# Two attentions and their neighbours: norms two turns ahead of their transposes, paced additions and paced first weights

## The chip, the cores and the metric

The kernel runs on one core of one Trainium2 chip. The metric is the device time of one execution in microseconds. A core has TensorE (PE; "PEld" is its weight load, which overlaps the products), VectorE (DVE), ScalarE (ACT), GpSimd (POOL) and SyncE (SP). Each engine works through its own list of instructions in order and waits at an instruction until the semaphores it names are reached. SP and POOL here also issue DMA transfers (SP for loads and stores, POOL for the gathers by index).

## The reference

Four layers, each with an attention against a context and a feed-forward part; x has 32 batches of 64 rows of 128 numbers, in float32. What matters here:

```python
# layer 1, feed-forward: each row goes to its two best of 8 experts
weights, indices = jax.lax.top_k(gates, 2)
out = jnp.sum(gathered * softmax(weights)[..., None], axis=2)
# layer 2, attention: 16 heads of 8, with a mask of keys
energy = where(mask == 0, -1e20, einsum('nhqd,nhkd->nhqk', q, k))
attn = softmax(energy / sqrt(8)); out = concat(attn @ v) @ Wo.T + bo
# layer 2, feed-forward: a soft mixture of 64 experts with 32 slots each
logits = einsum('bmd,dnp->bmnp', x, phi)
dispatch = softmax(logits, axis=0); combine = softmax over all (n, p)
y = einsum('bnpd,nde->bnpe', slots, W) + b
# layer 3: the same attention with biases, without the mask
# layer 3, feed-forward: 6 experts, two of them weighed in
h = gelu(einsum('btd,edh->bteh', x, w1)); out = einsum('bteh,ehd,bte->btd', h, w2, w)
# and throughout
x = x + part(_layernorm(x))
```

## The kernel before

**Tiles.** The 2048 rows are 16 tiles of 128 rows, in four groups (`NG` 4) of four tiles (`TG` 4). `X[g]` holds a group, 128 x 4 x 128, on chip from end to end. A norm of a group (`norm`, from L141) is on DVE: 4 statistics, 4 aggregations, 12 operations on 128 x 4 numbers for the reciprocal root, and 4 scalings (L157). `norm_T` (L166, L175) transposes its four tiles on PE and copies the result from PSUM on ACT.

**Attention of layers 2 and 3** (`attention16`). One function makes both, in 19 turns. In turn i, PE makes the scores of tile i (L1522 the mask, L1533), then the transposes of the exponentials of tile i-2 (`turn_e`, L166), then the values of tile i-3 (L1571). DVE takes the largest score of each row (L1542) and subtracts it (L1544), ACT makes the exponential in place (L1545) and copies the transposes (L1556). The scores lie in one of two PSUM tiles of two banks each (`banks2`), so the scores of a tile wait until L1544 of the tile two before is through. The logits of the mixture take the same two.

Beside this, steps for a group are put into a list `later` by turn: the queries of group g (norm and POOL's `add_row`, L793, in turn 4g-3; its transposes in 4g-2; the product with Wq, L1298, and ACT's copy or bias, L1301 and L1303, in 4g-1), the loads of the keys and values of group g+1 in turn 4g (`load_kv`: one load for the values and 16 for the keys, all on SP), the projection of group g in turns 4g+7 and 4g+8 (L777 or L779, L784; it ends with the addition to `X[g]`, L180, on DVE), and from turn 4g+8 on, one to a turn, what the caller gives with `after(g)`. Steps of turns past the last are issued one after the other behind the turns; that part is called the tail here.

- In layer 2, `after` is `first_logits(g)`: norm, an empty turn, transposes, and the first of the mixture's eight chunks of logits (`logits`, L1450 on PE, L1459 on DVE, L1465 and L1469 on ACT).
- In layer 3, `after` is `experts3(g)`: norm, an empty turn, transposes, `gate` (L1930, then some 15 small operations on DVE and an exponential on ACT, L1010), `hidden` (L1949 on PE, the Gelu on ACT, L1956), `weigh` (transposes L1023, copy L1025, products L1963, copies L1966 on ACT and products L1967 on POOL, or L1969 on DVE for the last group) and `project` (L1975, L180, and the store of the result on SP, L1983).

The caller of layer 2 also gives `before`: things to issue ahead of the scores of a turn.

**The gathered outputs of layer 1.** `fetch(g, k)` is one indirect DMA from POOL (L1223): 128 rows of an expert's output, one of eight for a group. `add_up_tokens(g)` adds the eight to `X[g]`, with their weights, on DVE (L1238). Groups 2 and 3 are fetched in the first turns of attention 2 and added in turns 4 and 8. A fetch is `paced`: it carries a wait on the last score product issued so far (`pe_at`).

**The first weights of the mixture.** `load_experts(c)` loads 8 of the 64 expert matrices, 512 KB, on SP (L1443) into one of three buffers. Chunks 0 and 1 are issued ahead of attention 2, chunk 2 after it.

**Order.** PE's list in the turns is exactly the order in which the function issues it: `in_order` binds each instruction behind the one before. The lists of DVE, ACT, POOL and SP, and PE's list in the tail, are put in order by the framework's planner, which takes the instructions by priority (the order of issue) as its own estimates say that they become ready. An instruction that is issued early can thus stand in DVE's list ahead of one that is ready sooner on the chip.

Of the kernel before, what the change touches and what calls it, by code (L numbers as in the profile page):

```python
# [20 lines left out]
ALU = mybir.AluOpType  # L21
# [30 lines left out]
def tile_layers(ctx: ExitStack, tc: tile.TileContext, io, out):  # L52
    nc = tc.nc
# [54 lines left out]
    def paced(ins):  # L108

        if pe_at[0] is not None:  # L110
            tc.add_manual_dep(
                ins.ins,
                pe_at[0].ins.name,
                mybir.DependencyInfo(mybir.DependencyClass.Sync, mybir.DependencyReason.DATA),
                reason="pace",
            )
# [378 lines left out]
    with tc.tile_pool(name="dtw", bufs=1, reuse_waits="tile") as dp:  # L495
# [131 lines left out]
        for i in range(S):  # L627
# [12 lines left out]
            if i % 16 == 15:  # L640
                q = i // 16
# [588 lines left out]
            )  # L1230
        )

    def add_up_tokens(g):
        wk = share.pop(g)[1]
        yg = ys.pop(g)
        for t in range(TG):
            for c in range(2):
                nc.vector.scalar_tensor_tensor(  # L1238
                    X[g][:, t, :], yg[c][:, t, :], wk[:, t, c : c + 1], X[g][:, t, :], ALU.mult, ALU.add
                )  # L1240


# [197 lines left out]

    def load_experts(c):
        wsm[c] = fa.tile([P, 8, D], F32, tag="wsm", name=f"wsm{c}", bufs=3)
        nc.sync.dma_start(wsm[c], io["W"][c * 8 : c * 8 + 8].rearrange("n p e -> p n e"))  # L1443

    def logits(c, g):

        ps = banks2(f"l{c}_{g}")
        psv = ps.rearrange("p (t s) -> p t s", t=TG)
        for k in range(TG):
            nc.tensor.matmul(  # L1450
                psv[:, k, :],
                xT2[g][:, k * P : (k + 1) * P],
                phi[:, c * CS : (c + 1) * CS],
                start=True,
                stop=True,
            )
        at = slice(g * TG, (g + 1) * TG)
        if c == 0:
            nc.vector.tensor_reduce(nmr[:, c, at], psv, AX.X, ALU.max, negate=True)  # L1459
        else:  # L1460
            rm = small.tile([P, TG], F32, tag="f2_rm", name=f"rm{c}_{g}")
            nc.vector.tensor_reduce(rm, psv, AX.X, ALU.max, negate=True)  # L1462
            nc.vector.tensor_tensor(nmr[:, c, at], rm, nmr[:, c - 1, at], ALU.min)  # L1463
        lg = fa.tile([P, TG, CS], F32, tag="lg", name=f"lg{c}_{g}", bufs=7)
        nc.scalar.copy(lg.rearrange("p t s -> p (t s)"), ps)  # L1465
        e = fa.tile([P, TG, CS], F32, tag="e", name=f"e{c}_{g}", bufs=4)
        for k in range(TG):
            t = g * TG + k
            nc.scalar.activation(e[:, k, :], psv[:, k, :], AF.Exp, bias=nmr[:, c, t : t + 1])  # L1469
        lgs[c, g], es[c, g] = lg, e  # L1470

        if g == 1:
            m = fa.tile([P, TG, CS], F32, tag="cm", name=f"cm{c}")
            nc.vector.tensor_tensor(m, lgs[c, 0], lg, ALU.max)
            cmx[c] = m
        elif g > 1:
            nc.vector.tensor_tensor(cmx[c], cmx[c], lg, ALU.max)
# [13 lines left out]
    def first_logits(g):  # L1491
        def normalise():
            xl2[g] = norm(g, "n5")

        def turn_over():
            xT2[g] = norm_T(g, "n5", xl2[g])[1]

        return [normalise, lambda: None, turn_over, lambda: logits(0, g)]

    load_experts(0)  # L1500
    load_experts(1)

    def attention16(ly, q16, wo, bv=None, mask=None, after=None, before={}):

# [3 lines left out]
        with tc.tile_pool(name=f"a{ly}", bufs=2, reuse_waits="tile", side="right") as aw:  # L1512
# [77 lines left out]

            for g in range(NG):
                if g:
                    for k, step in ((-3, normalise), (-2, turn_over), (-1, lambda g: queries(g, aw, "q"))):
                        later.setdefault(4 * g + k, []).append(lambda step=step, g=g: step(g))
                if 0 < g < NG - 1:
                    later.setdefault(4 * g, []).append(lambda g=g: load_kv(ly, g + 1, kv16[ly]))

                later.setdefault(4 * g + 7, []).append(
                    lambda g=g: later.setdefault("po", project_steps(g, os_[g], wo, f"a{ly}po{g}", bv))[0]()
                )  # L1600
                later.setdefault(4 * g + 8, []).append(lambda: later.pop("po")[1]())
                for k, step in enumerate(after(g)):
                    later.setdefault(4 * g + 8 + k, []).append(step)
# [17 lines left out]
    with tc.tile_pool(name="mask", bufs=1, reuse_waits="tile", side="right") as mp:  # L1621
        mi = mp.tile([P, NT, S], I32, name="mi")
        nc.sync.dma_start(mi, io["mask"].rearrange("(t p) k -> p t k", p=P))
        mb = mp.tile([P, NT, S], BF16, name="mb")
        nc.vector.tensor_scalar(mb, mi, 0.0, -1e20, ALU.is_equal, ALU.mult)
        identb = mp.tile([P, P], BF16, name="identb")
        nc.vector.tensor_copy(identb, ident)
        attention16(2, q2, wat[:, 7, :], mask=(identb, mb), after=first_logits,
            before={
                1: lambda: [fetch(2, k) for k in range(4, 8)],  # L1630
                2: lambda: [fetch(3, k) for k in range(4)],
                4: lambda: [fetch(3, k) for k in range(4, 8)] + [add_up_tokens(2)],
                8: lambda: add_up_tokens(3),
            },
        )

    kv_stack.close()
# [280 lines left out]
    def experts3(g):  # L1918
        v = {}

        def normalise():
            v["xl"] = norm(g, "n7")

        def turn_over():
            v["xT"] = norm_T(g, "n7", v["xl"])[1]

        def gate():
            ps = bank(f"z{g}")
            for t in range(TG):
                nc.tensor.matmul(  # L1930
                    ps[:, t * 6 : t * 6 + 6], v["xT"][:, t * P : (t + 1) * P], pw, start=True, stop=True
                )
            q = fp.tile([P, TG, 6], F32, tag="q", name=f"q{g}")
            nc.scalar.activation(
                q.rearrange("p t e -> p (t e)"), ps[:, : TG * 6], AF.Tanh, scale=1.0 / 0.3
            )
            pr = fp.tile([P, TG, 6, 6], F32, tag="pr", name=f"pr{g}")
            nc.vector.tensor_tensor(pr, _bc(q, 2, 6), _bc(anchors, 1, TG), ALU.mult)
            lg = fp.tile([P, TG, 6], F32, tag="lg", name=f"lg3_{g}")
            nc.vector.tensor_reduce(lg, pr, AX.X, ALU.add)  # L1940
            nc.vector.tensor_scalar(lg, lg, -6.0, 0.5, ALU.add, ALU.mult)
            nc.vector.tensor_scalar(lg, lg, rt, None, ALU.mult)
            v["w"] = top2(lg, 6, con[:, C_T6 : C_T6 + 36], fp, f"tk3_{g}")[1]

        def hidden():
            hw = v["hw"] = fp.tile([P, 3, 512], F32, tag="hw", name=f"hw{g}")
            for c in range(3):
                ps = bank(f"h3_{g}_{c}")
                nc.tensor.matmul(  # L1949
                    ps,  # L1950
                    w1[:, 2 * c : 2 * c + 2, :].rearrange("p e f -> p (e f)"),
                    v["xT"],
                    start=True,
                    stop=True,
                )
                nc.scalar.activation(hw[:, c, :], ps, AF.Gelu_apprx_tanh)  # L1956

        def weigh():
            wT = weights_T(v["w"], 6, fp, f"tk3_{g}", nc.scalar.copy)
            for c in range(3):  # L1960

                ps = bank(f"w3_{g}_{c}")
                nc.tensor.matmul(ps, sel[:, c * P : (c + 1) * P], wT, start=True, stop=True)  # L1963
                if g < NG - 1:
                    wh = fp.tile([P, 512], F32, tag="wh", name=f"wh{g}_{c}")
                    nc.scalar.copy(wh, ps)  # L1966
                    nc.gpsimd.tensor_tensor(v["hw"][:, c, :], v["hw"][:, c, :], wh, ALU.mult)  # L1967
                else:
                    nc.vector.tensor_tensor(v["hw"][:, c, :], v["hw"][:, c, :], ps, ALU.mult)  # L1969

        def project():
            ps = bank(f"o3_{g}")
            for t in range(TG):
                for c in range(3):
                    nc.tensor.matmul(  # L1975
                        ps[:, t * D : (t + 1) * D],
                        v["hw"][:, c, t * P : (t + 1) * P],
                        w2[:, c, :],
                        start=(c == 0),
                        stop=(c == 2),  # L1980
                    )
            add_to(g, ps)
            nc.sync.dma_start(o_rows[g], X[g])  # L1983

        return [normalise, lambda: None, turn_over, gate, hidden, weigh, project]

    kv16[3] = kv_buffers(3, ctx)
    for g in range(2):
# [106 lines left out]
```

## Time and profile before

| | us |
|---|---|
| median of 3 runs | 1115.15 |
| lowest and highest | 1106.98, 1124.36 |
| the profiled execution, its own time | 1120.74 |
| its span in the trace | 1119.0 |
| mean granted clock of PE | 0.88 |
| layer 1's experts end, attention 2 begins | about 445 |
| attention 2, last values end | about 560 |
| mixture, 8 chunks | about 582 to 950 |
| attention 3, its last values end | 1075 |

All times in the trace count from the start of the span. The page first gives each engine's busy time as a share of the span, then the span in 40 slices (28 us each): a digit is the busy share in tenths, and PEclk is the share of its clock that PE was granted. In the timeline a line has its start, its duration, engine, line of code, operation, tiles (written <- read), shapes and how often; in brackets stands how long the engine had been idle and what ended that ("issue": nothing that the profile shows; "remote": a semaphore whose sender it does not know). The windows view has, for each stretch, the length and then each engine's busy time with its number of instructions.

### The profile page before, as it was taken

Reading aid. Unit: us, or ns where it says so; the run is one execution under the profiler, and the core shown is the slowest. Engines: PE = TensorE matmul, PEld = TensorE weight load, DVE = VectorE, ACT = ScalarE, POOL = GpSimd, SP = SyncE. Lnnn points to the kernel's source line nnn. Section 1 sums busy time; section 2 is a strip of 40 time slices with the busy share of each in tenths; the row PEclk is TensorE's granted clock in tenths of the full one; section 3 lists DMA queues with packets and bytes.
Section 4 is the critical chain, followed back from the end, with each engine's and each line's share of the span. In section 5 each row is a group of like instructions: output and inputs, shape, how many; then the busy total and the mean of one; then the engine's idle time right before and its main releaser. Section 6 shows DMA issues by size and latency. Waiting matters only on the chain.

```text
span 1119.0 us, 26304 instructions
## 1 busy us (share of the span) xinstructions
PE 930.6 (83%) x10816; PEld 689.7 (62%) x10816; DVE 766.3 (68%) x2098; ACT 576.9 (52%) x987; POOL 151.7 (14%) x176
## 2 busy tenths in 40 slices
PE   5687679976789998597955989999999998697887
PEld 3455543455657776254644778888888887364554
DVE  8796897767555355456657876887788856867543
ACT  5544526664243454344525775776766733265552
POOL 3500020001053652500000000000000000300111
PEclk9867979989579999778867999999999999598887
DMA  6734030013312231310000000000000000220000
GB/s 229 169 123 151 35 138 8 20 45 102 107 47 46 69 71 52 103 29 4 1 1 1 2 21 2 21 21 2 22 21 2 3 3 3 75 63 2 10 10 19
DMA packets 63124, 51.89 MB, mean 46 GB/s; under 512 B 32663, under 2 KB 53541, under 8 KB 62878
## 3 DMA queue, kind: packets, MB, share of 16 engines
q1 hardware_dynamic: 46958, 29.86, 9.5%
q0 software_dynamic: 4368, 10.92, 3.6%
q10 hardware_dynamic: 11680, 9.44, 2.6%
q8 instruction: 86, 1.41, 0.5%
q14 instruction: 32, 0.26, 0.1%
HBM read 33.51 MB, written 15.60 MB: 44 GB/s over the span
## 4 chain that ended last, share of the span: by engine, by line
PE 56%; DVE 22%; ACT 11%; issue 4%; DMA 4%; POOL 1%; SPq 1%; ACTq 0%; another core or an unknown queue 0%; POOLq 0%; DVEq 0%
PE y L1728 7%; PE po L1747 5%; PE s L1708 4%; PE h L1339 3%; PE a_s L1533 3%; PE y L1361 3%; PE l L1450 3%; PE a_o L1571 2%; DVE lg L1698 2%; PE a_T L166 2%; PE h L893 2%; PE et L1671 2%; PE h1T_T L166 2%; PE w L1963 2%; DVE rm L1462 1%
## 5 line engine op out<-in xcount | busy, mean ns | idle before, releaser
L1728 PE MATMUL y<-wsm,sl 128*32 128x128 f32 x4096 | 118.4, 273 | 2.5 <-ACT sl L1716 2.5
L1728 PEld LDWEIGHTS y<-wsm,sl 128*32 128x32 f32 x4096 | 109.8, 110 | 10.7 <-issue 6.3
L1716 ACT COPY sl<-s 128x1024 f32<-128x1024 f32 x64 | 62.1, 1023 | 69.2 <-PE s L1708 69.2
L1351 ACT ACTIVATE hT<-h1T_T,b_t 128x128 f32<-128x128 f32 x184 | 52.6, 369 | 63.7 <-PE h1T_T L166 53.5
L793 POOL TENSOR_TENSOR X<-X,rows 128x512 f32<-128x512 f32 x8 | 10.2, 1271 | 496.1 <-DVE a3n_xl L157 435.2
L1542 DVE TENSOR_REDUCE a_x<-a_s 128x16 f32<-128x1024 f32 x32 | 39.0, 1217 | 55.9 <-PE a_s L1533 49.7
L1747 PE MATMUL po<-ybuf,cT 128*64 128x136 f32 x1024 | 66.4, 282 | 7.5 <-ACT e L1469 7.3
L1450 PE MATMUL l<-phi,n_xT 128*128 128x256 f32 x256 | 64.7, 408 | 3.5 <-ACT sl L1716 2.8
L1747 PEld LDWEIGHTS po<-ybuf,cT 128*64 128x64 f32 x1024 | 58.3, 137 | 14.2 <-ACT e L1469 8.7
L1708 PE MATMUL s<-lg,n_xl 64*128 64x256 f32 x512 | 65.1, 389 | 0.5 <-ACT e L1469 0.3
L166 PE MATMUL n_T<-con,n_xl 128*128 128x128 f32 x80 | 22.1, 370 | 50.7 <-DVE n_xl L157 30.9
L1556 ACT COPY a_eT<-a_T 128x512 f32<-128x512 f32 x64 | 35.2, 591 | 49.4 <-PE a_T L166 42.8
L1450 PEld LDWEIGHTS l<-phi,n_xT 128*128 128x128 f32 x256 | 50.8, 204 | 15.3 <-issue 4.0
L1761 DVE SCALAR_TENSOR_TENSOR acc<-acc,fac,po 128x128 f32<-128x128 f32 x112 | 31.3, 340 | 41.5 <-PE po L1747 41.5
L1465 ACT COPY lg<-l 128x1024 f32<-128x1024 f32 x32 | 32.6, 1020 | 46.7 <-DVE rm L1462 36.5
L1343 DVE COPY hs<-h 128x512 f32<-128x512 f32 x46 | 31.5, 687 | 35.2 <-PE h L1339 20.3
L1708 PEld LDWEIGHTS s<-lg,n_xl 64*128 64x128 f32 x512 | 47.6, 186 | 12.4 <-issue 5.6
L1204 POOL DMA_INDIRECT xg<-xn_dram,tok_u x46 | 43.7, 951 | 74.9 <-DVE tok_u L1178 30.3
L1339 PE MATMUL h<-w1e,xgT 128*128 x92 | 50.5, 637 | 0.8 <-issue 0.7
L166 PEld LDWEIGHTS a_T<-con,a_e 128*128 128x128 f32 x256 | 32.6, 159 | 29.4 <-issue 20.6
L1545 ACT ACTIVATE a_e<-a_e 128x1024 f32<-128x1024 f32 x32 | 33.8, 1058 | 32.6 <-DVE a_e L1544 26.2
L1469 ACT ACTIVATE e<-l,nmr 128x256 f32<-128x256 f32 x128 | 50.2, 501 | 0.4 <-DVE nmr L1463 0.4
(406 smaller groups left out, 2193.5 us busy)
## 6 DMA issues: line engine op xcount, KB each, us to landing
vd<-vb ACTq DMA_DIRECT2D x8, 576.0 KB
wsm<-in_W SPq DMA_DIRECT2D x8, 512.0 KB
y_dram<-ys SPq DMA_DIRECT2D x10, 256.0 KB
a2vb<-vd SPq DMA_DIRECT2D x4, 576.0 KB
a3vb<-vd SPq DMA_DIRECT2D x4, 576.0 KB
w1e<-in_W POOLq DMA_DIRECT2D x4, 512.0 KB
w2e<-in_W POOLq DMA_DIRECT2D x4, 512.0 KB
ctxT<-in_ctxT SPq DMA_DIRECT2D x4, 256.0 KB
```

Source lines behind the costliest of these rows:

```text
L166: nc.tensor.transpose(ps[:, t * P : (t + 1) * P], a, ident)
L1204: nc.gpsimd.indirect_dma_start(gathered[m][:, t, :], None, xn_dram[h][:], bass.IndirectOffsetOnAxis(ap=phase[h]["tok"][:, j : j + 1], axis=0),
L1339: pe_at[0] = nc.tensor.matmul(po, xgT[m][:, t * P : (t + 1) * P], w1f[:, bass.ds(at_e[m][t], 512)], start=True, stop=True)
L1351: nc.scalar.activation(hT[n][:, c, :], ps[:, c * P : (c + 1) * P], AF.Silu, bias=phase[h]["b1"][:, c, j : j + 1])
L1450: nc.tensor.matmul(psv[:, k, :], xT2[g][:, k * P : (k + 1) * P], phi[:, c * CS : (c + 1) * CS], start=True, stop=True,)
L1469: nc.scalar.activation(e[:, k, :], psv[:, k, :], AF.Exp, bias=nmr[:, c, t : t + 1])
L1542: nc.vector.tensor_reduce(mx, scv, AX.X, ALU.max)
L1556: nc.scalar.copy(eT[:, 4 * half : 4 * half + 4, :].rearrange("p k r -> p (k r)"), ps)
L1708: nc.tensor.matmul(ps[r][:, k * CS : (k + 1) * CS], xl2[g][half, k, :], lgs[c, g][half, k, :], start=True, stop=True,)
L1716: nc.scalar.copy(sl[:, r].rearrange("p q s -> p (q s)"), ps[r])
L1728: nc.tensor.matmul(pyv[(n % 4) * 32 : (n % 4) * 32 + 32, b, n // 4, :], sl[:, b % 2, 2 * h + b // 2, n * 32 : n * 32 + 32], wsm[c][:, n, : ...
L1747: nc.tensor.matmul(pov[r * 64 : r * 64 + 64, k // 2, k % 2, :], cT[:, j, at : at + 64], y[:, 2 * k + r, j, :], start=(j == 0), stop=(j == 1),)
```

## The change

- **Norms.** In `attention16` the norm for the queries of group g comes in turn 4g-4 instead of 4g-3, except for the group named by the new argument `late` (group 2, in layer 2). `first_logits` and `experts3` get a second empty turn between norm and transposes, so that their later steps come a turn later; `experts3` gets one more between `hidden` and `weigh`.
- **Gathered outputs.** `add_up_tokens` takes a function to apply to each addition. Group 2's are issued ahead of turn 5 instead of 4, group 3's ahead of turn 7 instead of 8, and both are `paced`: each addition waits for the last score product before it. The last four fetches are issued ahead of turn 3 instead of 4.
- **First weights.** `load_experts` 0 and 1 are no longer issued ahead of attention 2 but, paced, ahead of its turns 8 and 12.

```diff
-    def add_up_tokens(g):
+    def add_up_tokens(g, when=lambda ins: None):
...
-                nc.vector.scalar_tensor_tensor(
-                    X[g][:, t, :], yg[c][:, t, :], wk[:, t, c : c + 1], X[g][:, t, :], ALU.mult, ALU.add
+                when(
+                    nc.vector.scalar_tensor_tensor(
+                        X[g][:, t, :], yg[c][:, t, :], wk[:, t, c : c + 1], X[g][:, t, :], ALU.mult, ALU.add
+                    )
                 )
...
-        return [normalise, lambda: None, turn_over, lambda: logits(0, g)]
-
-    load_experts(0)
-    load_experts(1)
+        return [normalise, lambda: None, lambda: None, turn_over, lambda: logits(0, g)]
...
-    def attention16(ly, q16, wo, bv=None, mask=None, after=None, before={}):
+    def attention16(ly, q16, wo, bv=None, mask=None, after=None, before={}, late=None):
...
-                    for k, step in ((-3, normalise), (-2, turn_over), (-1, lambda g: queries(g, aw, "q"))):
+                    for k, step in ((-3 if late == g else -4, normalise), (-2, turn_over), (-1, lambda g: queries(g, aw, "q"))):
...
-                4: lambda: [fetch(3, k) for k in range(4, 8)] + [add_up_tokens(2)],
-                8: lambda: add_up_tokens(3),
+                3: lambda: [fetch(3, k) for k in range(4, 8)],
+                5: lambda: add_up_tokens(2, paced),
+                7: lambda: add_up_tokens(3, paced),
+                8: lambda: paced(load_experts(0)),
+                12: lambda: paced(load_experts(1)),
             },
+            late=2,
         )
...
-        return [normalise, lambda: None, turn_over, gate, hidden, weigh, project]
+        return [normalise, lambda: None, lambda: None, turn_over, gate, hidden, lambda: None, weigh, project]
```

More of the change, by code (lines that the diff above doesn't have):

```diff
@@ L1442, in load_experts @@
         wsm[c] = fa.tile([P, 8, D], F32, tag="wsm", name=f"wsm{c}", bufs=3)
-        nc.sync.dma_start(wsm[c], io["W"][c * 8 : c * 8 + 8].rearrange("n p e -> p n e"))
+        return nc.sync.dma_start(wsm[c], io["W"][c * 8 : c * 8 + 8].rearrange("n p e -> p n e"))
     def logits(c, g):
```

## The prediction

> **What bounds the kernel now.** I read the page first: its engine totals and slices, to see which engine is short in the two attentions.
>
> ```profile
> PE 930.6 (83%) x10816; PEld 689.7 (62%) x10816; DVE 766.3 (68%) x2098; ACT 576.9 (52%) x987; POOL 151.7 (14%) x176
> ...
> PE   5687679976789998597955989999999998697887
> ...
> PEclk9867979989579999778867999999999999598887
> ```
>
> PE (TensorE) carries the end, but slices 17 to 22 (attention 2 and the turn into the mixture) and 35 to 40 (attention 3) are mostly short of busy time, of clock or of both. Then the busy time by stretch: attention 2 is 445 to 560 us, its tail to 586; attention 3 starts at 952, and its tail at 1075.
>
> ```profile
> core 0: us, PE busy (x) PEld busy (x) DVE busy (x) ACT busy (x) POOL busy (x), PEclk, DMA share, GB/s
> 445.00:507.00 62.00, 45.94 (x387) 24.42 (x387) 33.26 (x75) 21.92 (x31) 16.46 (x17) 0.78 0.24 65
> 507.00:560.00 53.00, 43.87 (x488) 30.07 (x487) 34.05 (x99) 24.83 (x41) 1.54 (x2) 0.84 0.01 2
> ...
> 975.00:1005.00 30.00, 27.73 (x334) 18.06 (x331) 20.37 (x23) 18.34 (x27) 0.00 (x0) 0.96 0.21 61
> 1005.00:1075.00 70.00, 58.35 (x550) 37.19 (x548) 42.28 (x151) 37.93 (x56) 8.52 (x7) 0.82 0.02 5
> 1075.00:1119.00 44.00, 34.02 (x144) 23.19 (x142) 18.06 (x63) 14.08 (x22) 4.20 (x4) 0.77 0.06 18
> ```
>
> No engine fills these stretches: PE is idle 16, 9, 12 and 10 us of rows 1, 2, 4 and 5, and at 0.77 to 0.84 of its clock while busy. Row 3 shows what turns cost undisturbed: PE 92% busy at 0.96. So the two attentions are bound by short waits of PE, whose order is fixed there, and by the slow clock around them. The timeline says which waits. At the start:
>
> ```profile
> 454.98 0.38 DVE L1238 SCALAR_TENSOR_TENSOR X<-yg,wk,X 128x128 f32<-128x128 f32 x1 [3.18 <-issue]
> 455.28 1.21 DVE L1544 TENSOR_TENSOR a_e<-a_s,a_x 128x1024 f32<-128x1024 f32 x1
> ...
> 456.55 0.61 PE L1522 MATMUL a_s<-mb,identb 128*128 128x512 bf16 x2 [2.74 <-remote]
> ```
>
> The first addition of a gathered output stands in DVE's order before that turn's `a_e`; its gather has not landed, so `a_e` and the score bank it frees are 3 us late. Then the norms, on PE alone:
>
> ```profile
> 510.49 1.11 PE L1571 MATMUL a_o<-a2vb,a_eT 128*64 128x18 f32 x32
> 514.42 1.16 PE L166 MATMUL n_T<-con,n_xl 128*128 128x128 f32 x4 [2.81 <-DVE n_xl L157]
> 517.02 1.16 PE L166 MATMUL a2n_T<-con,a2n_xl 128*128 128x128 f32 x4 [1.45 <-DVE a2n_xl L157]
> ...
> 528.87 1.50 PE L1533 MATMUL a_s<-a2kb,a2qT 64*64 64x512 f32 x8 [2.58 <-ACT a2qT L1301]
> ```
>
> Two norms' transposes stand in turn 10 and wait for DVE, which has no gap over 0.5 us from 504.6 to 517.6; the queries of turn 11 then wait behind the first logits' copies on ACT. Last, the end of attention 3:
>
> ```profile
> 1040.28 5.48 PE L1963 MATMUL w<-tk_wT,sel 6*128 6x512 f32 x6 [2.64 <-ACT tk_wT L1025]
> ...
> 1068.69 4.61 PE L1963 MATMUL w<-tk_wT,sel 6*128 6x512 f32 x6 [0.67 <-ACT tk_wT L1025]
> ...
> 1073.23 1.90 PE L1571 MATMUL a_o<-a3vb,a_eT 128*64 128x18 f32 x32
> 1075.06 5.22 PE L1975 MATMUL o<-w2x,hw 128*128 128x128 f32 x24
> ...
> 1082.30 0.63 PE L166 MATMUL a3po_T<-con,a3o 128*128 128x128 f32 x4
> ```
>
> Group 1's `weigh` (w) and `project` (o) stand before and after the last values (a_o), and group 3, whose chain ends the kernel, starts its projection only at 1082.30 though its input was ready at 1075.99.
>
> **The change, part by part.** No instruction is added or removed; instructions change place, and some get a wait on PE.
>
> *Additions.* Group 2's eight go from turn 4 to 5, group 3's from turn 8 to 7, each behind the last score product. 8 x 0.344 = 2.75 us of DVE a group. The wait of 2.74 us at 456.55 goes: gain 2.7 (0 to 2.7). Behind the waiting additions DVE holds `a_x`, `a_e` and the norm of their group. Group 2's norm stays in turn 5 (late=2), directly behind them, and its transposes in turn 6 already wait 1.94 us, at the end of 3.9 us of DVE on the chain of waits (486.17 to 490.11). What hid the additions was DVE's idle time at 459 to 485; that cover is partly gone: loss 0 to 2.75, taken 1.5.
>
> *Gathers.* POOL issues 16 (16 x 0.95, 1.25 apart, 20 us) without a break but one; the last four being called in turn 3 instead of 4 moves nothing on POOL's queue: 0. The additions of group 3 need the last of them, about 472, before turn 7.
>
> *First weights.* Two loads of 512 KB, and the third, which in the trace goes out with them (2.55 us of SP from 446.25), go to turns 8 and 12, unless the third stays early. On SP they now stand among the 16 key loads of turn 4 (461.61 to 472.8) and of turn 8 (494.09 to 505.6); a load is about 512 KB / 300 GB/s = 1.7 us there, against 20 us until turn 12 wants the keys, and the mixture reads wsm at 620: 0. Behind a paced load SP holds group 3's values and keys, which wait for PE's same turns anyway. In the old place they fill 446 to 453 (up to 342 GB/s), and the gather issued at 448.77 serves its addition only at 454.98 (6.2 us; 2.5 for the one issued at 426.93). After that PE shows gaps "issue" in an `a_o` and a score product, 0.99+2.29+1.27+1.21+3.50 = 9.3 us at 459.9 to 473.4, with every engine still. Gathers and key loads, which stay, run just there; key loads alone (978.9 to 990) leave turns of 3.1 us undisturbed. So the part of wsm is open: 0 to 9.3, I take 4, under half.
>
> *Norms one turn earlier or later.* Group 3's query norm comes in turn 8 instead of 9, POOL's add_row (1.27) with it, and the first logits' transposes in turn 11 instead of 10. DVE's work to turn 10 is the same (two norms of 4.9, three pairs of 2.45), so only n's part is given a turn more: the waits were 2.81+1.45 = 4.3; gain 0 to 4.3, taken 2. The logits in turn 12 leave ACT free for the queries: gain 0 to 2.6, taken 2. Group 1's transposes (waited 2.14 at 545.91) go to turn 15: gain 0 to 2.1, taken 2. In attention 3, turn 10 has the same pair of waits, 3.79+1.44 = 5.2: taken 2.5 (0 to 5.2). Group 1's query norm in attention 2 was done at 439.1, and groups 1 and 2's in attention 3 at 967.6, all before the turns: 0.
>
> *Clock.* Of the 137 us from 445 to 582 the clock is 0.79, so 2 x 0.21 x 137 = 58 us are at half speed; a score product then takes 1.99 instead of 1.09. A gap is followed by about 7 us of it (0.92, 0.50, 0.73 in windows of 4 us from 486: 0.6+4+2.2 us), costing up to 3.4. Some three gaps fewer: 0 to 10, taken 4. [...]
>
> *Mixture of layer 3.* Gate and `hidden` come one turn later, `weigh` two. In turn 13 PE waited 2.64 for tk_wT, behind ACT's Gelus, exponentials and table loads, and then ran w in 5.48 at half clock, where six like products of `hidden` take 2.84: gain 0 to 5.3, taken 3.5. At the end, group 1's w (4.61, with 1.2 for its transposes and copy) leaves the place before the last values and its o (5.22) the place before group 3's projection; both go into the tail beside group 3's norm (6.4 us of DVE), with the three POOL products (3 x 1.26). If all of it is covered, 11 us are won; if the tail is full of PE work (34.0 of 44 busy), its 10 us of gaps take it only in part; and it may push group 3's chain back by w and o, 9.8. Taken 6 (-9.8 to 11). A switch of ACT's table is 1.28 us in the rows, the next instruction 0.01 us behind; none is counted as gone. [...]
>
> **Sum.** 2.7 - 1.5 + 4 + 2 + 2 + 2 + 2.5 + 4 + 3.5 + 6 = 27.2 us. The profiled execution took 1120.74 us (span 1119.0), so 1093.5 by it. It lies 5.6 over the median of 1115.15; less 27.2 the median gives 1088. I take 1092, nearer to the first, since a good part of its excess may be the stall at 460 to 473 of which 4 are counted.
>
> **Rivals.** (1) *The tail takes it back.* PE in the tail gets w and o, 9.8 us, and if the gaps there do not take them, the end moves by as much as the turns won: the last term is 0 instead of 6, half of the clock's term goes (2), and the pair of waits in turn 10 stays (4.5), as a norm is finished only when DVE is through with both: 27.2 - 12.5 = 14.7, about 1104 by the same reading. For it: DVE without a gap at 504 to 517. Against: group 3's chain waited 6.3 us for PE. (2) *Waits only move.* The additions and norms have the same producers; the gap that goes comes back one turn on: within 5 us of before, 1112. (3) *Wsm's collision was the stall:* all of 9.3, and half of the 9 us of half-clock work behind it (4.5): 9.8 more than the sum, 1082. (4) *Slower: DVE in turns 5 to 10.* Additions of 2.75 a group move out of DVE's idle stretch to just before three norms; if both lie in full on the path, with 3.4 of slow clock behind each, and nothing of the norms is won, 2 x 6.15 = 12.3 less the 2.7: 9.6 slower, 1125. It decides where DVE's work from turn 5 to 10 exceeds PE's by more than a turn. Against: DVE is busy only 33.26 of 62 us to 507.
>
> **How the numbers follow.** Forecast 0.46 (own range 1082 to 1102), rival 1 0.16, rival 2 0.10, rival 3 0.14, rival 4 0.14. Two per cent is 22.3 us, about what a measurement of this kernel can tell from no change. Faster needs 1092.8: rival 3 and over half of the forecast, 0.40. Slower needs 1137.5, rival 4 with a second such stretch in attention 3: 0.08. Within 2%: 0.52. The range: upward to rival 4, 1125; downward the sum with every term at its best is (9.3-4) + (4.3-2) + (2.6-2) + (5.2-2.5) + (10-4) + (5.3-3.5) + (11-6) + 1.5 = 25.2 more, 1067; I cut that at 1072.
>
> **What would show it.** Right: no DVE wait over 1 us before the first L1238 addition; `wsm` issued after the scores of turns 7 and 11; n_T of the logits a turn behind a2n_T, and no ACT wait before turn 12's scores; PEclk over 0.85 in both stretches; a3po_T of group 3 within 2 us of the last a_o. Wrong: the stall at 460 to 473 is still there, a2n_T of group 2 waits over 4 us, or PE idles as long in the tail with its end no earlier.

## The result and the profile after

| | before | after |
|---|---|---|
| median, four runs each (us) | 1118.99 | 1128.51 |
| lowest and highest | 1106.98, 1124.36 | 1126.90, 1129.23 |
| profiled execution, span | 1120.74, 1119.0 | 1126.90, 1124.8 |

The ratio, which compares fast executions alone and so need not be the quotient of the medians, is 1.0125 [1.0076, 1.0174]: about 1% slower, where 1092 us had been forecast, 2.1% under the 1115.15 known then. The page of the changed kernel, its engine totals and the granted clock:

```profile
PE 933.1 (83%) x10816; PEld 695.9 (62%) x10816; DVE 761.5 (68%) x2098; ACT 576.5 (51%) x987; POOL 152.2 (14%) x176
...
PEclk9777789988579999788967999999999999698866
```

The work is the same; the last two slices fell from 0.8 and 0.7 to 0.6 and 0.6. The busy time by stretch, cut as before, 3.4 us later (attention 2 in two rows, the last part of attention 3, the tail):

```profile
core 0: us, PE busy (x) PEld busy (x) DVE busy (x) ACT busy (x) POOL busy (x), PEclk, DMA share, GB/s
448.40:510.40 62.00, 41.78 (x382) 22.43 (x382) 32.52 (x75) 21.21 (x31) 16.41 (x17) 0.83 0.17 47
510.40:563.40 53.00, 42.89 (x510) 30.17 (x507) 38.04 (x118) 24.76 (x42) 2.17 (x3) 0.88 0.08 22
...
1008.40:1067.00 58.60, 48.49 (x484) 32.55 (x484) 34.34 (x113) 32.55 (x48) 5.06 (x4) 0.83 0.02 6
1067.00:1124.80 57.80, 44.08 (x158) 28.75 (x154) 17.13 (x76) 18.54 (x29) 7.59 (x6) 0.70 0.05 14
```

The last row is the result: the tail is 57.8 us instead of 44.0, with 44.1 us of PE in it instead of 34.0, at 0.70 of the clock instead of 0.77. Its timeline, where *w* and *o* are the weigh and project of a group (first group 1's, then group 2's) and `a3po_T` and the additions to X from `a3po_o` belong to group 3:

```profile
1066.10 1.11 PE L1570 MATMUL a_o<-a3vb,a_eT 128*64 128x18 f32 x32
...
1069.68 1.01 PE L1023 MATMUL tk_T<-con,tk_w 128*6 128x128 f32 x4 [2.46 <-DVE tk_w L1016]
1071.36 5.48 PE L1966 MATMUL w<-tk_wT,sel 6*128 6x512 f32 x6 [0.67 <-ACT tk_wT L1025]
...
1077.67 1.06 PE L166 MATMUL a3po_T<-con,a3o 128*128 128x128 f32 x4
1078.53 4.84 PE L1978 MATMUL o<-w2x,hw 128*128 128x128 f32 x24
...
1085.27 0.69 DVE L180 TENSOR_TENSOR X<-X,a3po_o 128x512 f32<-128x512 f32 x1 [0.20 <-PE a3po_o L784]
...
1095.89 1.11 PE L166 MATMUL n_T<-con,n_xl 128*128 128x128 f32 x4
...
1098.98 4.49 PE L1978 MATMUL o<-w2x,hw 128*128 128x128 f32 x20
1103.31 0.28 PE L1933 MATMUL z<-pw,n_xT 128*128 128x6 f32 x2
```

PE's list in the tail puts other groups' work ahead of group 3's chain twice: group 1's w and o ahead of its projection, group 2's o ahead of the last products of its gate (z). Counted from the start of the last value product (1067.0; 1074.9 before), the addition of group 3's projection ends at 19.0 us (12.3 before, +6.6), the last of the four transposes of its n_T starts at 29.6 (20.2; +2.8 more; below, "n_T" with a time is this one), z ends at 36.6 (24.6; +2.6 more), the last product ends at 53.7 and the last addition at 54.4 (40.0 and 40.8; +1.7 more): 13.7. The sign that the prediction gave for its own failure in the tail is there (an end no earlier), and so are the other two, the stall and a2n_T of group 2, both below.

All stages, from the start of a stage's first score product to the start of its last value product (the tail runs to the end of the span, the mixture from attention 2's last values to attention 3's first score):

| us | start | attention 2 | mixture | attention 3 | tail | span |
|---|---|---|---|---|---|---|
| before | 446.6 | 113.7 | 403.0 | 111.6 | 44.1 | 1119.0 |
| after | 450.1 | 108.7 | 404.0 | 104.2 | 57.8 | 1124.8 |
| difference | +3.5 | -5.0 | +1.0 | -7.4 | +13.7 | +5.8 |

The start, 3.5 us, is not the change's: up to attention 2 every engine's list is the same, and in 18 traces of these kernels it takes 436 to 452 us. That goes with the granted clock: over the whole start it is 0.86 to 0.88 in the seven traces up to 447.5 us and 0.84 or 0.85 in the eleven from 448.0 on (0.86 before, 0.85 after), and at 76 to 112 us it is 1.00 in e1, whose start takes 436.4 us, against 0.71 before and 0.67 after.

### The profile page after: what moved, and what is told of

Read it like the earlier page. It is cut to its first block, busy times and chain, and to the rows that moved or that the text cites. A ratio compares the mean times of both kernels' runs of the same rounds, so it can differ in the third digit from the quotient of the medians.

```text
span 1124.8 us, 26303 instructions
## 1 busy us (share of the span) xinstructions
PE 933.1 (83%) x10816; PEld 695.9 (62%) x10816; DVE 761.5 (68%) x2098; ACT 576.5 (51%) x987; POOL 152.2 (14%) x176
## 4 chain that ended last, share of the span: by engine, by line
PE 57%; DVE 22%; ACT 10%; issue 4%; DMA 4%; POOL 1%; SPq 1%; ACTq 0%; DVEq 0%; POOLq 0%
PE y L1731 8%; PE po L1750 5%; PE s L1711 4%; PE a_s L1532 3%; PE h L1341 3%; PE l L1452 3%; PE y L1363 3%; PE a_o L1570 3%; PE a_T L166 2%; DVE lg L1701 2%; PE h L893 2%; PE et L1674 2%; PE w L1966 2%; PE h1T_T L166 2%; PE o L1978 2%
## 5 line engine op out<-in xcount | busy, mean ns | idle before, releaser
L1731 PEld LDWEIGHTS y<-wsm,sl 128*32 128x32 f32 x4096 | 111.5, 111 | 10.7 <-issue 6.3
L793 POOL TENSOR_TENSOR X<-X,rows 128x512 f32<-128x512 f32 x8 | 10.2, 1269 | 501.3 <-DVE a3n_xl L157 437.0
L1452 PEld LDWEIGHTS l<-phi,n_xT 128*128 128x128 f32 x256 | 51.8, 208 | 15.4 <-issue 4.0
L1363 PE MATMUL y<-w2e,hT 128*128 x368 | 49.6, 279 | 0.9 <-ACT hT L1353 0.9
```

Source lines behind the costliest of these rows:

```text
L1363: nc.tensor.matmul(yo[m][:, t * D : (t + 1) * D], a[:, c, :], w2f[:, bass.ds(at_e[m][t] + c * D, D)], start=(c == 0), stop=(c == 3),)
L1452: nc.tensor.matmul(psv[:, k, :], xT2[g][:, k * P : (k + 1) * P], phi[:, c * CS : (c + 1) * CS], start=True, stop=True,)
L1731: nc.tensor.matmul(pyv[(n % 4) * 32 : (n % 4) * 32 + 32, b, n // 4, :], sl[:, b % 2, 2 * h + b // 2, n * 32 : n * 32 + 32], wsm[c][:, n, : ...
```

## Experiments

Four kernels each were run on one chip together: e1 to e4, e5 to e8, e9 to e12, e13 to e16. Theory T: the later turns of layer 3's mixture are the loss.

### e1_mixture_turns_back and e12: the mixture of layer 3 in its old turns

```diff
-        return [normalise, lambda: None, lambda: None, turn_over, gate, hidden, lambda: None, weigh, project]
+        return [normalise, lambda: None, turn_over, gate, hidden, weigh, project]
```

> The changed kernel with the mixture of layer 3 in its old turns (the list of experts3 as before), all else as changed. Theory T (the later turns of layer 3's mixture push group 1's weigh and project into the tail, ahead of group 3's chain, and this costs more than its turns win): attention 3 from its first score to its last values takes about 111 us again (104.2 in the changed kernel), the tail behind it about 44 (57.8), so 6 less than the changed kernel: about 1122, and a few us under the kernel before run beside it if the rest of the change is worth the 5 us that attention 2 got shorter. Rival R (the loss lies ahead of attention 3, in the paced additions, the first weights or the norms): within 3 us of the changed kernel, 1126 to 1131.

> The changed kernel with the mixture of layer 3 in its old turns once more. T: tail 44.2 us, attention 3 at 111 to 112 us, ratio to before 0.995 to 1.001, where the rest of the change wins at most the 5 us of attention 2 (less on a chip that shows the stall at 460 to 475 us, which swallows the 3.4 us won in front of it: there 0.998 to 1.001).

Measured: 0.9976 [0.9942, 1.0011] and 1.0008 [0.9960, 1.0055]; tail 44.2 us in both, attention 3 111.7 and 111.5. One edit takes the loss away, on two chips, and what is left of the change has a ratio that can't be told from 1.

The chip of e1 shows something else. It has no stall in turn 3 of attention 2; these are the values of the first tile:

```profile
445.95 1.11 PE L1570 MATMUL a_o<-a2vb,a_eT 128*64 128x18 f32 x32
```

The same values on the chip of the changed kernel, and on e12's, come in single products with gaps, and the turn takes 21 us instead of 5 (16 in the kernel before). From the changed kernel:

```profile
472.96 0.19 PE L1570 MATMUL a_o<-a2vb,a_eT 128*64 128x18 f32 x1 [1.91 <-issue]
...
475.36 1.07 ACT L1555 COPY a_eT<-a_T 128x512 f32<-128x512 f32 x2 [13.18 <-remote]
```

### e2_mixture_turns_alone: only the new turns, on the kernel before

The edit is the reverse of the one above.

> The kernel before with only the new list of experts3 (an empty turn more between norm and transposes and one more ahead of weigh). Theory T: turns of attention 3 about 104 us (111.6 before), tail about 58 (44.1), so 5 to 8 slower than the kernel before: ratio 1.005 to 1.007. Rival R: the turns win and the tail loses nothing, ratio 0.99 to 1.00.

Measured: 1.0113 [1.0046, 1.0181], tail 57.7, attention 3 111.9. The part alone makes the whole loss. Its turns won nothing here, against the 104 us that were expected, though PE's order in them is the one that took 104.2 us in the changed kernel.

### e11_after_again

> The changed kernel once more, on the same chip as e12_mixture_turns_back_again, for the difference of the two. T: the tail is 57.8 us again whatever the chip; the difference of the two kernels' times is the 13.6 of the tail less what the turns of attention 3 win, which two traces put at 7.4 and two at 0 (104.2 and 104.4 us against 111.9 for the same order of PE): between 6 and 14 us. Ratio to before 1.008 to 1.013.

Measured: 1.0106 [1.0046, 1.0167], tail 57.8, attention 3 104.4; 8.6 us above e12 beside it (1129.77 against 1121.19), by stages 13.6 - 7.1 = 6.5.

### e10_no_turn_ahead_of_weigh

```diff
-        return [normalise, lambda: None, lambda: None, turn_over, gate, hidden, lambda: None, weigh, project]
+        return [normalise, lambda: None, lambda: None, turn_over, gate, hidden, weigh, project]
```

> The changed kernel without the empty turn ahead of weigh; the one between norm and transposes stays. Theory T (the loss goes with the work that is pushed behind the last values): group 1's w is back in front of the tail, its o and group 2's transposes are not; the tail is 48 to 52 us, between 44.2 and 57.8, and the time between the changed kernel and the one with both turns back: ratio 1.002 to 1.008. Rival (it is the transposes' turn alone that costs): tail at 56 or more, ratio 1.012.

Measured: 1.0108 [1.0062, 1.0153], tail 54.6: between the two cases, and over the 48 to 52 us and the 1.008 of theory T. The expectation had an error: group 1's weigh falls in turn 18, but there behind the values, so w and o still both stand ahead of group 3's projection (its addition ends at 19.2 us, as in the changed kernel). One empty turn already costs 10.4 of the 13.6 us.

### e3_mixture_turns_group0 and e16: the later turns for group 0 alone

```diff
-        return [normalise, lambda: None, lambda: None, turn_over, gate, hidden, lambda: None, weigh, project]
+        more = [lambda: None] * (g == 0)
+        return [normalise, lambda: None] + more + [turn_over, gate, hidden] + more + [weigh, project]
```

> The changed kernel with the two empty turns of layer 3's mixture for group 0 alone; groups 1 to 3 have the old turns, so PE's list behind the last values is that of the kernel before. Theory T: the tail is 44 us again and a part of the 7.4 us of the turns stays (group 0's weigh no longer in turn 13): 1113 to 1120, 8 to 14 under the changed kernel. If the 7.4 came from group 1's transposes and gate being later, the turns are at 110 and it is about 1121. Rival R: within 3 us of the changed kernel.

> The kernel e3_mixture_turns_group0 once more (0.9931 on the chip without the stall), for a ratio on the chip that the other three of this call run on. On a chip with the stall: attention 2 at 109, attention 3 at 106 to 107, tail 45, ratio 0.992 to 0.998 if the kernel before has 113.7, 111.6 and 44.1 there; about 1.000 if its usual execution is shorter than that.

Measured: 0.9931 [0.9894, 0.9967] and 0.9899 [0.9863, 0.9934]; attention 3 106.6 and 106.8, tail 45.2 and 45.3. Both chips are without the stall. So a version beats both kernels there, by under 2%. Beside e1, with no later turn, e3's turns are 5.1 us shorter and its tail 1.0 longer; beside e11, with later turns for every group, the two e3 traces' turns are 2.2 to 2.4 us longer and their tails 12.5 to 12.6 shorter. The loss came with the groups behind group 0, whose steps fall off the end. The times do not tell e3 from e1, which ran beside it: the medians are 1097.81 and 1094.93. Nor does the gain show on a chip with the stall: e8 below, which has e3's attention 3, gave 1.0011.

### e15_before_group0_turns

The same list on the kernel before.

> The kernel before with the two empty turns of layer 3's mixture for group 0 alone. If the gain in turns 12 to 15 of attention 3 (111.6 to 106.6 us in e3_mixture_turns_group0) is its own: tail 45 us, ratio 0.994 to 0.998. If it hangs on the clock that happens to be granted there: attention 3 anywhere from 106 to 118 us, ratio 0.998 to 1.005.

Measured: 0.9980 [0.9932, 1.0027], attention 3 115.2, tail 44.6. PE's order in attention 3 is that of e3 and e16, and it takes 8.5 us more: PE is busy for 97.9 us at 0.78 of its clock there, against 89.0 us at 0.85 in e3. So this gain hangs on the clock granted there.

### e4, e6 and e9: the order in the tail

e4 issues, with the turns as changed, all steps of the last group ahead of the others' of the same turn; its projection's two steps both in turn 19:

```diff
-                later.setdefault(4 * g + 8, []).append(lambda: later.pop("po")[1]())
...
+                    if last:
+                        later.setdefault(4 * g + 7, []).insert(k, step)
...
-                    later.setdefault(4 * g + 8 + k, []).append(step)
+                    at = later.setdefault(4 * g + 8 + k, [])
+                    at.insert(0 if last else len(at), step)
```

> The changed kernel, all turns as changed, but in layer 3 the steps of the last group (its projection first) are issued ahead of the other groups' steps of the same turn in the tail, so that PE has its projection directly behind the last values and its norm's transposes ahead of group 2's w. Theory T (the place of group 1's w and o ahead of the projection is the loss): X of group 3 is added to some 7 us after the last values instead of 19, n_T of group 3 about 7 us earlier, the tail 46 to 51 us instead of 57.8: 1116 to 1122. Rival C (the tail is bound by the sum of PE's work at a low clock, not by its order): the tail stays at 55 or more and the time within 3 us of the changed kernel.

Measured: 0.9997 [0.9951, 1.0043], tail 51.6; the addition of group 3's projection ends at 5.5 us (19.0), n_T starts at 19.4 (29.6). T is borne out, if just over its 46 to 51 us: with the same work in the tail, the order alone gives back 6.2 of the 13.7 us. With the other 7.5 goes more work: PE is busy in this tail for 41.3 us, and for 34.1 in that of the kernel before.

e6 has e4's order with group 0's turns (e3), and the project of groups 1 and 2 a turn later:

```diff
+        none = lambda: None
+        more, late1 = [none] * (g == 0), [none] * (g in (1, 2))
+        return [normalise, none] + more + [turn_over, gate, hidden] + more + [weigh] + late1 + [project]
```

> A version meant to beat both: later turns of layer 3's mixture for group 0 alone, and behind the last values the steps of the last group ahead of the others', with the project of groups 1 and 2 a turn later. If the tail is set by the chain of the last group and PE's work ahead of it (theory T): attention 3's turns at 106 to 107 us as in e3_mixture_turns_group0, the addition to X of group 3 ends 6 to 8 us after the last values (11.9 in the kernel before), tail 38 to 42 us (44.1, 45.2); ratio to before about 0.988 to 0.990. If the tail is bound by the sum of its work on PE, it stays at 44 to 46 and the ratio is 0.993.

Measured: 1.0006 [0.9966, 1.0046], tail 47.1, attention 3 114.8. The projection's addition ends at 5.8 us, about as expected (the kernel before has 12.3, not the 11.9 named there), but n_T only starts at 22.9: now group 1's o and group 2's z, h and w stand ahead of it, at 0.68 of the clock.

e9 moves these too (and has the additions of e5):

```diff
+        n = lambda: None
+        if g == 2:
+            return [normalise, n, turn_over, n, lambda: (gate(), hidden()), n, n, n, weigh, n, project]
+        if g == 3:
+            return [normalise, turn_over, gate, hidden, n, weigh, n, project]
...
```

> A version meant to beat both: the attention of layer 2 as changed, with group 2's additions ahead of turn 4; in layer 3 the later turns for group 0 alone, and PE's list behind the last values written by hand: the last group's projection first, then group 1's o and group 2's z and h beside the last group's norm, then the last group's n_T, z and h, and only then w and o of groups 2 and 3. If the tail is set by the order (T): n_T of group 3 starts 13 to 16 us after the last values (20.2 in the kernel before, 22.9 in e6_last_first_and_group0), tail 36 to 41 us (44.1), ratio to before 0.985 to 0.993. If it is bound by the sum of PE's work at its clock (C): n_T comes earlier but the tail stays at 43 to 47, ratio 0.995 to 1.000.

Measured: 0.9985 [0.9940, 1.0029], tail 46.7 (the profiled execution took 1127.29 us, the second longest of twelve; the median is 1119.75). n_T starts at 13.5 us and z ends at 15.5, 9 us earlier than in the kernel before, and the end is not earlier (the last product ends at 42.6, 40.0 before). One reason is a wait:

```profile
1096.89 0.60 PE L1023 MATMUL tk_T<-con,tk_w 128*6 128x128 f32 x4
1097.82 1.28 ACT L1010 ACT_TABLE_LOAD   x1
1099.35 1.28 ACT L1966 ACT_TABLE_LOAD   x1
1101.14 0.56 ACT L1025 COPY tk_wT<-tk_T 6x512 f32<-6x512 f32 x1
1101.75 5.49 PE L1973 MATMUL w<-tk_wT,sel 6*128 6x512 f32 x6 [4.26 <-ACT tk_wT L1025]
```

tk_T is done at 1097.5, but ACT alternates between the gate's exponentials (L1010) and the Gelus (L1966), loads a table for each, and copies tk_wT only at 1101.14; PE waits 4.26 us, and both w that follow run at half clock (5.49 and 5.48; two of e4's three w take 2.84). But the wait is the smaller part. From the end of z to the last product PE takes 27.1 us here and 15.4 in the kernel before, because group 2's w and o, which stood ahead of z there, now stand behind it: a second w of 5.48, and 7.19 for two groups' o instead of 4.84 for one, are 7.8 of the 11.7 us; the waits for w grew from 3.1 to 4.9. C's numbers hold: the work was moved, not won. The alternation costs ACT four table loads of 1.28 us from 1093.29 to 1100.63, two of them above. No kernel here was run with the exponentials and the Gelus grouped, so what that would win is not shown.

### e5_additions_turn4

Based on e3:

```diff
-                5: lambda: add_up_tokens(2, paced),
+                4: lambda: add_up_tokens(2, paced),
```

> The kernel with the later turns for group 0 alone (e3_mixture_turns_group0), and group 2's additions, still waiting for a score product, ahead of turn 4 instead of 5. Theory T2 (what the additions' wait won at turn 3, 3.4 us, was lost again at turn 6, because group 2's norm, behind its own additions and mixed with group 3's, kept a2n_T waiting 5.75 us): the wait of a2n_T falls under 3 us, turn 7 starts 27 to 29 us after turn 0 instead of 30.7, and attention 2 to its last values takes 89 to 91 instead of 92.3. Rival W (the additions in turn 4 wait for their gathers, or the waits only move on): turn 7 at 30 to 32 us, attention 2 at 92 or more.

Measured: 0.9996 [0.9950, 1.0042], on a chip with the stall: turn 7 starts at 43.7 us, attention 2 takes 105.9; beside it, with turn 5, 46.9 and 109.4 (e8). 3.2 and 3.5 us are won, as T2 said (its figures were for a chip without the stall). First the changed kernel's wait for group 2's norm and, above it, DVE's list there (the last line is group 3's wait in turn 10); then e5's wait:

```profile
491.65 0.15 DVE L130 SCALAR_TENSOR_TENSOR a2n_r_u<-a2n_r_t,a2n_v 128x4 f32<-128x4 f32 x1
491.73 0.34 DVE L1239 SCALAR_TENSOR_TENSOR X<-yg,wk,X 128x128 f32<-128x128 f32 x1
...
494.68 1.15 PE L166 MATMUL a2n_T<-con,a2n_xl 128*128 128x128 f32 x4 [5.28 <-DVE a2n_xl L157]
...
520.62 1.16 PE L166 MATMUL a2n_T<-con,a2n_xl 128*128 128x128 f32 x4 [5.23 <-DVE a2n_xl L157]
```

```profile
481.56 1.01 PE L166 MATMUL a2n_T<-con,a2n_xl 128*128 128x128 f32 x4 [2.29 <-DVE a2n_xl L157]
```

From 491.4 us on, an addition of group 3 (0.34) stands between each two small operations (0.15) of group 2's norm. The time of e5 did not follow the 3.5 us: its attention 3 took 118.6 us, for which see the last section.

### e7_first_logits_back and e8_weights_ahead

Based on e3; e7 takes the second empty turn out of `first_logits`, e8 issues the first weights ahead of attention 2 again, without a wait:

```diff
-        return [normalise, lambda: None, lambda: None, turn_over, lambda: logits(0, g)]
+        return [normalise, lambda: None, turn_over, lambda: logits(0, g)]
```

```diff
+    load_experts(0)
+    load_experts(1)
...
-                8: lambda: paced(load_experts(0)),
-                12: lambda: paced(load_experts(1)),
```

> As e3_mixture_turns_group0, but first_logits with one empty turn between norm and transposes, as before. Theory T3 (all that attention 2 won, about 5 us, is won in turns 11 to 15, by the logits a turn later): attention 2 to its last values 96 to 98 us, as in the old order (97.0), and turn 11 starts as before at 56 to 57. Rival (it is group 3's query norm, a turn earlier, that won it): stays at 92 to 94.

> As e3_mixture_turns_group0, but the mixture's first two weight loads ahead of attention 2 again, without a wait. Theory T4 (the loads' place is worth nothing; the stall of 460 to 475 us that the first two profiles show is not theirs): attention 2 to its last values within 1.5 us of 92.3, mixture and attention 3 unchanged, time within 3 us of e3_mixture_turns_group0 (ratio 0.990 to 0.996). Rival (they cost what the forecast gave them): 4 to 9 us longer turns 3 to 6 of attention 2.

Measured, both with the stall, so that the times expected for a chip without it are missed: e8 1.0011 [0.9962, 1.0060], attention 2 109.4 us, against 109.6 in e6, which ran beside it with the loads in their new place. The loads' place is worth nothing, and the stall is there with either. e7 1.0064 [1.0029, 1.0099], attention 2 117.3; the scores of turn 11 start at 73.3 us in e7 and 73.2 in e8, those of turn 15 at 104.4 and 95.5. e7 has the two waits of the kernel before again (2.58 and 2.14 there):

```profile
530.45 2.40 PE L1532 MATMUL a_s<-a2kb,a2qT 64*64 64x512 f32 x8 [2.58 <-ACT a2qT L1303]
548.78 1.00 PE L166 MATMUL n_T<-con,n_xl 128*128 128x128 f32 x4 [2.15 <-DVE n_xl L157]
```

The changed kernel has 0.87 for the first and nothing for the second. 3.9 us of waits are gone, and with the half clock behind them (the `a_T` that follows the first takes 1.97 us in e7 and 1.09 in e8) the stretch from turn 11 to turn 15 is 8.8 us shorter. T3 holds.

### e13_before_alone and e14: the kernel before, unchanged

> The kernel before itself, for a second profile of it. If its one trace is typical: start 440 to 450 us, attention 2 to its last values 113 to 114 us on a chip that shows the stall (97 on one that does not), attention 3 at 111 to 112, tail 44. Rival (its one trace was a poor execution, and the 5 us of attention 2 are not won on average): attention 2 under 110 us on a chip with the stall.

> The same for a third profile: as for e13_before_alone, and the two within 1 us of each other in attention 2, attention 3 and tail if what differs from execution to execution lies in the start alone.

Measured, on a chip without the stall: start 449.2 and 449.3, attention 2 99.6 and 96.2, attention 3 111.6 and 115.6, tail 44.1 and 44.2. The rival falls as far as this chip tells: without the stall the old order takes 96.2 to 99.6 us in four traces, the new one 92.3 to 93.0 in four. The two executions agree in the start, against the expectation, and differ in the two attentions, by 3.4 and 4.0 us.

## Why the prediction was wrong, point by point

- *The tail ("Taken 6 (-9.8 to 11)")* is the step that failed. It had group 1's o leave "the place before group 3's projection" and put w and o beside group 3's norm; PE ran both ahead of the projection, and the tail became 13.7 us longer. The prediction named the mechanism, "it may push group 3's chain back by w and o", and then weighed it against gaps of 10 us. It did not write down PE's list behind the last values: group 1's weigh (turn 19) is issued in the same turn as group 3's projection, ahead of it. And it counted one push; there were two, with group 2's o ahead of z, and a lower clock on top (0.70 instead of 0.77). The term also counts what the turns win when w leaves them. Later turns for the groups behind group 0 (e3 against the changed kernel) win 2.4 us there and cost 12.6 in the tail: -10.2 where the sum has +6. That is 16 us of the forecast's error, and a little more than the term's own low end.
- *Wsm and the stall, 4*: 0 (e8). Rival 3 falls with it. The stall goes with the chip, or with the time at which that chip was used: it is in the first pair and in all of e5 to e12, in none of e1 to e4 and e13 to e16, old lists and new on either side. What makes it was not found.
- *Additions' wait, 2.7*: right, 3.0 us at turn 3 (10.5 to 7.5). On a chip with the stall 1.2 of it is left at turn 5 (33.8 to 32.6).
- *Group 2's norm, -1.5*: right in sign, too small: the wait went from 1.94 to 5.28, -3.3 (2.29 in e5). The additions of group 3 were not counted against it.
- *Turn 10, 2 and 2.5*: both 0. In attention 2 one wait of 5.23 stands where there were 2.81 and 1.45; turn 10 takes 10.3 us (10.5). In attention 3 it is one of 6.20; 10.5 (10.6). Rival 1's reason, that DVE is through with both norms only then, was right.
- *Queries behind the logits, 2, and group 1's transposes, 2*: right and too small. The waits were 1.7 and 2.1; with the clock behind them (0.50 from 531 to 537 us in the kernel before, where the `a_T` after the first wait took 1.97 us; 1.09 in the changed one) the stretch from turn 11 to turn 15 became 6.2 us shorter (28.3 to 22.1).
- *Not counted*: the same later logits reach into the mixture, which takes 402.5 to 403.0 us with the old list of `first_logits` and 404.0 to 404.8 with the new: -1.0 in the pair.
- *Weigh out of turn 13, 3.5*: 4.1 by e3 against e1 (turns 5.1 shorter, tail 1.0 longer), so near the mark there. But e15 has e3's order at 115.2 us, and e2 has the changed kernel's at 111.9 instead of 104.2: the gain comes and goes with the clock (0.78 in e15 and 0.85 in e3, 0.76 in e2 and 0.83 in the changed kernel, over attention 3), so that the size was in part luck.
- *Clock, 4*: 0.80 to 0.87 over attention 2, 0.77 to 0.70 in the tail, 0.88 to 0.875 over the whole: moved, not won.

The mechanism that decided was rival 1's, "the tail takes it back", only that the tail took 13.7 us and the turns of attention 3 had won 7.4. Rival 4, the slower case, gave 1125 and so came near the time by another road, which is luck: DVE in turns 5 to 10 cost the 3.3 above, not 9.6. By stages, without the start, the change costs 2.3 us; the ratio says 14. The medians lie 9.5 apart, and the traces 6. The four times of the kernel before lie 17 us apart, and one trace of each kernel can't stand for them; what the rest is no stage of these traces shows, and it stays open.

## What to carry to other kernels

A step that is given one turn more is also pushed past the end of the turns for the last groups: write down the list of the engine behind the last turn, instruction by instruction, before giving a price, and give the extra turn only to groups that have turns left. Work that is moved to a tail has to be priced by what it stands in front of, not by the gaps the tail has. An order by hand that clears the front of the chain moves the work behind it: in e9 a product of the chain came 9 us earlier, and the work and the waits that now followed it took that back.

## What the runs showed of the hardware

The clock behind one and the same gap. PE's order in attention 3 is the same in e3 (first) and e5 (second):

```profile
981.29 1.53 PE L1532 MATMUL a_s<-a3kb,a3qT 64*64 64x512 f32 x8 [1.44 <-ACT a3qT L1305]
...
983.78 1.11 PE L1570 MATMUL a_o<-a3vb,a_eT 128*64 128x18 f32 x32
```

```profile
985.97 1.50 PE L1532 MATMUL a_s<-a3kb,a3qT 64*64 64x512 f32 x8 [1.44 <-ACT a3qT L1305]
...
988.94 1.90 PE L1570 MATMUL a_o<-a3vb,a_eT 128*64 128x18 f32 x32
990.78 2.08 PE L784 MATMUL a3po_o<-wat,a3po_oT 128*128 128x128 f32 x8
```

After the same wait of 1.44 us PE went on at full speed in e3 (granted clock 1.00 in the windows from 981 to 989); in e5 it ran at half speed from about 988 us to 994.7, some 7 us (granted clock 0.50 in the windows from 988 to 994). Over attention 3, e3 takes 106.6 us, with PE busy for 89.0 us at 0.85 of its clock; e5 takes 118.6, with 101.8 us at 0.76. Kernels that were run twice on different chips mostly came out alike: 104.2 and 104.4 for the changed order, 106.6 and 106.8 for e3's, 111.7 and 111.5 for e1's. But the kernel before gave 111.6 twice and 115.6 in e14, on the chip of e13. And one order of PE in different programs gave 104.2 to 111.9 (the changed kernel, e4, e11, e2) and 106.6 to 118.6 (e3, e16, e8; e5 to e7, e9, e15). So a stage of a few microseconds' gain can't be told from the clock by one trace of each kernel. What sets the clock's pattern is not shown.
